# Scaled xi copied to PSUM by TensorE as the source of ScalarE's products, in a kernel of pairwise outer products with batch normalization

## The chip, the cores and the metric

The kernel runs on one core of a Trainium2 chip. Its metric is the device time of one execution in microseconds. The times below are of three executions and of one more under the hardware profiler. "ACT" is ScalarE, "DVE" VectorE, "PE" TensorE, "POOL" GpSimd and "SP" SyncE, which issues all stores.

## The reference

There are two inputs xi and xj of 1024 x 39 x 16, a 16 x 16 weight W, and gamma and beta of 741 entries. For every pair of fields (row r, column c) with c < r, 741 pairs in all, and for every batch element, the outer product of xj's field r and xi's field c is formed, normalized by mean and variance over the batch and over its 256 entries, scaled and shifted, and multiplied by W element by element. The output is 1024 x 1 x 741 x 16 x 16 in fp32, 776.99 MB.

```python
cross = xj[:, rows, :, None] * xi[:, cols, None, :]
mean = jnp.mean(cross, axis=(0, 2, 3), keepdims=True)
var = jnp.mean(jnp.square(cross - mean), axis=(0, 2, 3), keepdims=True)
normed = (cross - mean) * jax.lax.rsqrt(var + BN_EPS)
normed = normed * gamma[None, :, None, None] + beta[None, :, None, None]
out = normed[:, :, None, :, :] * W[None, None, :, :, :]
```

## The kernel before

**Layout.** Batch element 8p + t lies on partition p, so there are eight values of t on each of 128 partitions. A *tile* is one row r (or two short rows) for two values of t: 2r pairs of 256 entries on each partition. `y_sb` holds 152 pairs and is reused in turn: a tile's products can only be written where earlier stores have landed. The tuple of a tile in `FIRST` and `LAPS` (L19 to L32) is: the rows; how many of the 16 values of i POOL multiplies instead of ACT; how many pairs ("share") POOL finishes instead of DVE; whether ACT adds the shift for that share (1) or POOL (0); and how many pairs DVE finishes ahead for the first t alone. The 120 tiles are numbered in the order of the code: 0 to 3 are row 19, 4 to 11 rows 20 and 18 in turn, 12 to 15 row 38, and from 16 on longer rows come with short ones.

**Statistics.** Sixteen loads of 312 KB, one of them in two parts, bring in xi and xj; sums and squares on DVE, ACT, POOL and PE (L376 to L411) give two small matrices, from which scale and shift of all pairs follow (L476 to L489). PE spreads them over the partitions by matmuls (`spread`, L496, into PSUM), and `apply` (L512, three DVE operations a group) multiplies in gamma and adds beta, group of rows by group of rows (`ROW_GROUPS`, L46). A group is applied four tiles (group 2: three) before its first use (L537 to L540).

**The steps of a tile n.** `scale_xi` (L186, POOL, L193) multiplies xi by the scale into `xs`, of which there are two buffers. `products` (L201) forms xs times xj[i] for each of 16 values of i and each t: ACT does i below `split` (L170), POOL the others (L172); rows up to 5 go to POOL at once (L228), rows up to 4 to DVE (L209, L219). `finish` (L282) adds the shift and multiplies by W: POOL for its share (shift at L298 by ACT or L300 by POOL, weight at L303), DVE for all other pairs in one operation each (L319). `store` (L241) then sends the tile, or one t of it, to the output from SP (L246). Tile 1 (`RAW`) has a share of its own, `POOL_PAIRS_RAW` (L38), and the first three tiles a number of i of their own, `POOL_I_FIRST`.

**The order** is written out by hand (`manual_schedule`): for n = 1, 2, ... it is scale_xi(n + 2), finish(n), the groups that are due, products(n + 1). Each engine runs its instructions in that order.

**PSUM.** One bank holds W for DVE (`w_dve`), seven are `banks`; the first serve the statistics and, from tile 12 on, xj of the short rows (`xj_short`, ScalarE's copy at L551); the others hold the spread groups.

Of the kernel before, what the change touches and what calls it, by code (L numbers as in the profile page):

```python
# [7 lines left out]
F32 = mybir.dt.float32  # L8
# [6 lines left out]
T = 2  # L15
# [2 lines left out]

FIRST = ((19,), 5, 3, 0, 0)  # L19
LAPS = (  # L20
# [14 lines left out]
)  # L35


POOL_I_FIRST, POOL_PAIRS_RAW = (6, 6, 5), 2  # L38

SHORT, OWN = 4, 1  # L40


OUTER = 5
# [4 lines left out]
    (5, 10, 2), (25, 29, 3), (10, 14, 3), (21, 25, 4), (14, 18, 4),  # L48
)
SHORT_GROUP = 5  # L50


@with_exitstack
def tile_pair_outer_batchnorm(
# [15 lines left out]
    nc = tc.nc  # L70
    P = nc.NUM_PARTITIONS
    NB, F, E = xi.shape
    NT = NB // P
    EE = E * E
    NP = F * (F - 1) // 2
    first = [r * (r - 1) // 2 for r in range(F)]

# [4 lines left out]
    tiles = [(FIRST, t0, t0 // T * half // 2) for t0 in range(0, NT, T)]  # L82
    for lap in LAPS:
        size = T * sum(sum(member[0]) for member in lap)
# [12 lines left out]
    cpool = ctx.enter_context(tc.tile_pool(name="cpool", bufs=1))  # L97
    scaled_short = ctx.enter_context(tc.tile_pool(name="scaled_short", bufs=1))
    scaled = ctx.enter_context(tc.tile_pool(name="scaled", bufs=2))
    psp = ctx.enter_context(tc.tile_pool(name="ps", bufs=1, space=bass.MemoryType.PSUM))  # L100
    xi_sb = cpool.tile([P, NT, F, E], F32, name="xi_sb")
    xj_sb = cpool.tile([P, NT, F, E], F32, name="xj_sb")
    w_sb = cpool.tile([P, 1, EE], F32, name="w_sb")
    st_sb = cpool.tile([P, 2, NP], F32, name="st_sb")
    s_sb = st_sb[:, 0:1].unsqueeze(3)
    t_sb = st_sb[:, 1]
    y_sb = cpool.tile([P, 2 * half, EE], F32, name="y_sb")
    w_dve = psp.tile([P, 1, EE], F32, name="w_dve")

    xi_v = xi.rearrange("(p t) f e -> p t f e", t=NT)  # L110
    xj_v = xj.rearrange("(p t) f e -> p t f e", t=NT)
    out_v = out.rearrange("(p t) o n i j -> p t (o n i j)", t=NT)


# [1 line left out]
    flat = y_sb.rearrange("p n e -> p (n e)")  # L116
    place = {"mid": half // 2 * EE, "dev": half * EE, "rest": (half + half // 2) * EE}
    stop = {"mid": half * EE, "dev": (half + half // 2) * EE, "rest": 2 * half * EE}

    def scratch(part, parts, *shape):  # L120
        size = 1
        for n in shape:
            size *= n
        at = place[part]
        place[part] = at + size
        assert place[part] <= stop[part]
        ap = flat[0:parts, at : at + size]
        if len(shape) == 2:
            ap = ap.rearrange("p (a b) -> p a b", b=shape[1])
        elif len(shape) == 3:  # L130
            ap = ap.rearrange("p (a b c) -> p a b c", b=shape[1], c=shape[2])
        return ap

    G = F - 1
    H = E // 2
    squares = [scratch("dev", P, NT, G, E) for _ in range(2)]
    halves = [[scratch("mid", P, NT, G, H) for _ in range(2)] for _ in range(2)]
    ones = scratch("rest", P, P)  # L140
    unit = scratch("rest", P, P)
    pick = scratch("rest", G, G, P)
    moments = [scratch("rest", P, NT, 2 * G) for _ in range(2)]
    squared, low, rstd, inv = (scratch("rest", G, G) for _ in range(4))
    stq = scratch("rest", G, 2, G)
    banks = [psp.tile([P, 512], F32, name=f"ps{n}") for n in range(7)]
    ps_s, ps_c, ps_g = banks[0], banks[1], banks[2:5]

    xj_short = ps_c.rearrange("p (t r i) -> p t r i", t=NT, i=E)

    ps_st = banks[5:7] + ps_g
    stt = nc.vector.scalar_tensor_tensor
# [1 line left out]
    def view(n):  # L154
        (rows, *_), _, u = tiles[n]
        return y_sb[:, u : u + T * sum(rows), :].rearrange("p (t n) e -> p t n e", t=T)

    def parts(n):
        at = 0
        for r in tiles[n][0][0]:  # L160
            yield r, at, at + r
            at += r

    def product(n, r, at, engine, t, i, src):

        t0 = tiles[n][1]
        y = view(n)[:, t, at : at + r].rearrange("p n (i j) -> p n i j", j=E)[:, :, i, :]
        scale = xj_sb[:, t0 + t, r, i : i + 1]
        if engine is nc.scalar:
            nc.scalar.activation(y, src, AF.Copy, scale=scale)  # L170
        else:
            engine.tensor_scalar(y, src, scale, 1.0, ALU.mult, ALU.mult)  # L172
# [13 lines left out]
    def scale_xi(n):  # L186
# [11 lines left out]
            )  # L198
        xs_of[n] = xs

    def products(n):  # L201

        t0 = tiles[n][1]
        xs = xs_of.pop(n, None)
        for r, c0, c1 in parts(n):
            outer = view(n)[:, :, c0:c1].rearrange("p t n (i j) -> p t n i j", j=E)
            if r <= SHORT:
                xs_r = scaled_short.tile([P, T, r, E], F32, tag="xs_short", name=f"xs_{r}_{t0}")
                nc.vector.tensor_tensor(  # L209
                    xs_r,  # L210
                    xi_sb[:, t0 : t0 + T, 0:r, :],
                    s_short[:, first[r] : first[r] + r]
                    .unsqueeze(1)
                    .unsqueeze(3)
                    .to_broadcast([P, T, r, E]),
                    ALU.mult,
                )
                for t in range(T):
                    nc.vector.tensor_tensor(  # L219
                        outer[:, t],  # L220
                        xs_r[:, t].unsqueeze(2).to_broadcast([P, r, E, E]),
                        xj_short[:, t0 + t, r - 1 : r, :].unsqueeze(3).to_broadcast([P, r, E, E]),
                        ALU.mult,
                    )
                continue
            if r <= OUTER:
                for t in range(T):
                    nc.gpsimd.tensor_tensor(  # L228
                        outer[:, t],
                        xs[:, t, c0:c1].unsqueeze(2).to_broadcast([P, r, E, E]),  # L230
                        xj_sb[:, t0 + t, r : r + 1, :].unsqueeze(3).to_broadcast([P, r, E, E]),
                        ALU.mult,
                    )
                continue
            split = E - (POOL_I_FIRST[n] if n < len(POOL_I_FIRST) else tiles[n][0][1])
            for t in range(T):
                for i in range(E):
                    engine = nc.scalar if i < split else nc.gpsimd
                    product(n, r, c0, engine, t, i, xs[:, t, c0:c1])

    def store(n, c0, c1, t_from=0, t_to=T):  # L241
        (rows, *_), t0, _ = tiles[n]
# [2 lines left out]
        for t in range(t_from, t_to, step):  # L245
            nc.sync.dma_start(  # L246
                out_v[:, t0 + t : t0 + t + step, (n0 + c0) * EE : (n0 + c1) * EE],
                view(n)[:, t : t + step, c0:c1, :].rearrange("p t n e -> p t (n e)"),
# [85 lines left out]
    with tc.manual_schedule():  # L334
        nc.gpsimd.memset(ones, 1.0)  # L335

        def load(engine, to, source, t):
            engine.dma_start(to[:, t], source[:, t])

        nc.sync.dma_start(xi_sb[:, 0, 0 : F // 2], xi_v[:, 0, 0 : F // 2])  # L340
        nc.scalar.dma_start(xi_sb[:, 0, F // 2 : F], xi_v[:, 0, F // 2 : F])
        load(nc.sync, xj_sb, xj_v, 0)
        load(nc.scalar, xi_sb, xi_v, 1)
        load(nc.sync, xj_sb, xj_v, 1)
# [19 lines left out]

        sources = (xj_sb[:, :, 1:F], xi_sb[:, :, 0:G])
        scales = (0.25, 0.25 / NB**0.5)

        def field(x, k):  # L370
# [103 lines left out]
        scale = 1.0 / (NB * EE)  # L474
# [18 lines left out]
        spread_of = []  # L493
# [18 lines left out]
        def apply(group):  # L512
            ps, n0, n1 = spread_of[group]
            nc.vector.tensor_mul(ps[:, 1], ps[:, 1], st_sb[:, 0, n0:n1])
            if group == SHORT_GROUP:

                nc.vector.tensor_mul(ps[:, 0], ps[:, 0], st_sb[:, 0, n0:n1])
                nc.vector.tensor_copy(st_sb[:, 0, n0:n1], ps[:, 0])
            else:
                nc.vector.tensor_mul(st_sb[:, 0, n0:n1], ps[:, 0], st_sb[:, 0, n0:n1])  # L520
            nc.vector.tensor_add(st_sb[:, 1, n0:n1], ps[:, 1], st_sb[:, 1, n0:n1])

        spread(0)
        apply(0)

        affine(0, range(OWN, 12))
# [2 lines left out]
        weigh(0)  # L529
        for group in range(1, len(ROW_GROUPS)):  # L530
            spread(group)
        s_short = spread_of[SHORT_GROUP][0][:, 0]
        apply(1)
        products(1)
        scale_xi(2)

        due = {}  # L537
        for group, (r0, r1, _) in enumerate(ROW_GROUPS[2:], 2):
            use = min(n for n, tile in enumerate(tiles) if any(r0 <= r < r1 for r in tile[0][0]))
            due.setdefault(use - 3 if group == 2 else use - 4, []).append(group)  # L540

        for n in range(1, len(tiles)):
            if n + 2 < len(tiles):
                scale_xi(n + 2)
            finish(n)
            for group in due.get(n, ()):
                apply(group)
            if n + 1 < len(tiles):
                products(n + 1)
            if n == 12:  # L550
                nc.scalar.copy(xj_short, xj_sb[:, :, 1 : SHORT + 1, :])  # L551


# [26 lines left out]
```

## Time and profile before

| | us |
|---|---|
| median of 3 runs | 1863.21 |
| lowest and highest | 1863.09, 1863.3 |
| the profiled execution, its own time | 1863.2 |
| its span in the profile | 1861.1 |

| engine | busy us | share of the span |
|---|---|---|
| DVE | 1764.1 | 95% |
| POOL | 1593.2 | 86% |
| ACT | 1581.5 | 85% |
| PE | 33.1 | 2% |
| DMA queue of SP (16 DMA engines) | | 98.6% |

The mean rate of the DMA is 421 GB/s over the span: 6.00 MB are read and 776.99 MB written. The costliest groups are DVE's finish at L319 (3014 operations, 1703.0 us), ACT's products at L170 (3000, 1453.8 us) and POOL's products at L172 (1192, 635.9 us) and weights at L303 (131, 531.4 us).

A group's line gives the busy time, the mean of one operation in ns, and the idle time of its engine just before such operations with what ended it. A line of the waits gives who waited for whom: us in total, how often, the longest. A line of the operations in order of time gives start, length, engine, line, operation, how many are merged, and in brackets the idle time before. A line of a table by stretches gives, after the stretch, each engine's busy time with the number of operations (PE, PE's weight loads, DVE, ACT, POOL), PE's granted clock, the DMA's share and GB/s.

### The profile page before, as it was taken

The page shows a single profiled execution, that of the slowest core. Times are in us where ns is not written, and L with a number is a line of the kernel's source. Part 1 is how long each engine was busy: PE and PEld are TensorE (multiplying, and loading weights), DVE is VectorE, ACT ScalarE, POOL GpSimd, SP SyncE. Part 2 cuts the span into 40 slices and gives each one's busy share as a digit, 9 for nine tenths or more (in the row PEclk, how much of TensorE's full clock was granted, in tenths as well). Part 3 has the DMA queues.
Part 4 walks back from the last instruction along what each step waited for, and adds up shares of the span by engine and source line. Part 5 has one row for each costly group of instructions (what it writes and reads, how often), then busy time and mean ns, then how long its engine had stood idle before and what let it go on. Part 6 is the DMA issues. An engine that isn't in the chain of part 4 may idle for free. (4 is left out here: it accounts for less than half of the span.)

```text
span 1861.1 us, 10096 instructions
## 1 busy us (share of the span) xinstructions
PE 33.1 (2%) x212; PEld 32.3 (2%) x212; DVE 1764.1 (95%) x3141; ACT 1581.5 (85%) x3208; POOL 1593.2 (86%) x1810
## 2 busy tenths in 40 slices
PE   7000000000000000000000000000000000000000
PEld 6000000000000000000000000000000000000000
DVE  8999999998999999999999999899999999999894
ACT  8999888888888777779888888888888888888991
POOL 9989878888888799989888888999988888888791
PEclk7555555555555555555555555555555555555555
DMA  7999999999999999999999999999999999999998
GB/s 290 393 422 418 440 427 429 430 436 413 429 436 430 423 427 429 428 431 427 428 429 429 428 433 431 429 406 429 427 423 427 424 425 428 414 424 425 427 427 369
DMA packets 41356, 783.64 MB, mean 421 GB/s; under 512 B 4288, under 2 KB 4928, under 8 KB 11712
## 3 DMA queue, kind: packets, MB, share of 16 engines
q1 hardware_dynamic: 40992, 782.53, 98.6%
q14 instruction: 75, 0.61, 0.1%
q10 hardware_dynamic: 288, 0.48, 0.1%
q8 instruction: 1, 0.02, 0.0%
HBM read 6.00 MB, written 776.99 MB: 421 GB/s over the span
## 5 line engine op out<-in xcount | busy, mean ns | idle before, releaser
L319 DVE SCALAR_TENSOR_TENSOR y_sb<-y_sb,st_sb,w_dve 128x512 f32<-128x512 f32 (+1 forms) x3014 | 1703.0, 647 | 61.7 <-POOL y_sb L172 48.1
L170 ACT ACTIVATE y_sb<-xs,xj_sb 128x576 f32<-128x576 f32 (+23 forms) x3000 | 1453.8, 576 | 227.6 <-DMA out_dram<-y_sb 198.3
L172 POOL TENSOR_SCALAR y_sb<-xs,xj_sb 128x112 f32<-128x112 f32 (+27 forms) x1192 | 635.9, 557 | 6.2 <-DMA out_dram<-y_sb 4.9
L303 POOL TENSOR_TENSOR y_sb<-y_sb,w_sb 128x2048 f32<-128x2048 f32 (+4 forms) x131 | 531.4, 4063 | 71.3 <-ACT y_sb L298 63.7
L193 POOL TENSOR_TENSOR xs<-xi_sb,st_sb 128x640 f32<-128x640 f32 (+33 forms) x135 | 182.9, 1362 | 148.2 <-ACT y_sb L170 130.9
L300 POOL TENSOR_SCALAR y_sb<-y_sb,st_sb 128x512 f32<-128x512 f32 x300 | 202.2, 691 | 2.0 <-ACT y_sb L170 2.0
L298 ACT ACTIVATE y_sb<-y_sb,st_sb 128x512 f32<-128x512 f32 x168 | 105.1, 708 | 4.6 <-POOL y_sb L172 3.1
L219 DVE TENSOR_TENSOR y_sb<-xs,ps 128x256 f32<-128x256 f32 (+3 forms) x32 | 24.8, 817 | 0.5
L228 POOL TENSOR_TENSOR y_sb<-xs,xj_sb 128x1280 f32<-128x1280 f32 x8 | 18.7, 2364 | 0.0
L503 PE MATMUL ps<-y_sb 38*128 38x38 f32 (+37 forms) x76 | 15.3, 379 | 2.4 <-DVE y_sb L489 2.4
L503 PEld LDWEIGHTS ps<-y_sb 38*128 38x128 f32 x76 | 15.2, 310 | 2.5 <-POOL y_sb L172 2.5
L172 POOL TENSOR_SCALAR y_sb<-xi_sb,xj_sb 128x304 f32<-128x304 f32 x24 | 11.9, 515 | 0.0
L269 DVE TENSOR_TENSOR y_sb<-y_sb,w_dve 128x2048 f32<-128x2048 f32 (+4 forms) x6 | 10.8, 1840 | 0.5 <-POOL y_sb L262 0.5
L380 DVE TENSOR_REDUCE y_sb<-y_sb 128x38 f32<-128x608 f32 x14 | 10.4, 780 | 0.0
L262 POOL TENSOR_SCALAR y_sb<-y_sb,st_sb 128x512 f32<-128x512 f32 x9 | 7.0, 791 | 1.5 <-ACT y_sb L170 1.5
L377 ACT ACTIVATE y_sb<-xj_sb 128x608 f32<-128x608 f32 x8 | 5.7, 709 | 1.2 <-DMA xj_sb<-in_r_xj_dram 0.6
L377 ACT ACTIVATE y_sb<-xi_sb 128x608 f32<-128x608 f32 x8 | 5.7, 709 | 1.1 <-DMA xi_sb<-in_r_xi_dram 0.7
L260 ACT ACTIVATE y_sb<-y_sb,st_sb 128x512 f32<-128x512 f32 x9 | 6.5, 800 | 0.1
L395 PE MATMUL ps<-xi_sb,y_sb 128*128 128x152 f32 x40 | 5.8, 293 | 0.3 <-DMA xi_sb<-in_r_xi_dram 0.3
L417 PE MATMUL ps<-y_sb 128*128 128x128 f32 x24 | 5.4, 426 | 1.0 <-POOL y_sb L335 1.0
L395 PEld LDWEIGHTS ps<-xi_sb,y_sb 128*128 128x128 f32 x40 | 5.4, 190 | 0.5 <-issue 0.5
L380 DVE TENSOR_REDUCE y_sb<-xi_sb 128x38 f32<-128x608 f32 x2 | 1.6, 785 | 3.9 <-DMA xi_sb<-in_r_xi_dram 3.9
(43 smaller groups left out, 54.1 us busy)
## 6 DMA issues: line engine op xcount, KB each, us to landing
out_dram<-y_sb SPq DMA_DIRECT2D x16, 3968.0 KB, 19.5
out_dram<-y_sb SPq DMA_DIRECT2D x16, 3456.0 KB, 20.9
out_dram<-y_sb SPq DMA_DIRECT2D x16, 2944.0 KB, 20.3
out_dram<-y_sb SPq DMA_DIRECT2D x8, 4864.0 KB, 16.8
out_dram<-y_sb SPq DMA_DIRECT2D x8, 4736.0 KB, 18.4
out_dram<-y_sb SPq DMA_DIRECT2D x8, 4608.0 KB, 20.2
out_dram<-y_sb SPq DMA_DIRECT2D x8, 4480.0 KB, 17.0
out_dram<-y_sb SPq DMA_DIRECT2D x8, 4352.0 KB, 17.7
```

The source lines that it names most:

```text
L170: nc.scalar.activation(y, src, AF.Copy, scale=scale)
L172: engine.tensor_scalar(y, src, scale, 1.0, ALU.mult, ALU.mult)
L193: nc.gpsimd.tensor_tensor(xs[:, :, c0:c1, :], xi_sb[:, t0 : t0 + T, 0:r, :], s_sb[:, :, n0 : n0 + r, :].to_broadcast([P, T, r, E]), ALU.mult,)
L219: nc.vector.tensor_tensor(outer[:, t], xs_r[:, t].unsqueeze(2).to_broadcast([P, r, E, E]), xj_short[:, t0 + t, r - 1 : r, :].unsqueeze(3). ...
L228: nc.gpsimd.tensor_tensor(outer[:, t], xs[:, t, c0:c1].unsqueeze(2).to_broadcast([P, r, E, E]), xj_sb[:, t0 + t, r : r + 1, :].unsqueeze(3 ...
L298: nc.scalar.activation(y[:, :, c, :], y[:, :, c, :], AF.Identity, bias=t_c)
L300: nc.gpsimd.tensor_scalar(y[:, :, c, :], y[:, :, c, :], t_c, 1.0, ALU.add, ALU.mult)
L303: nc.gpsimd.tensor_tensor(y[:, :, c0:c1, :], y[:, :, c0:c1, :], w_sb.unsqueeze(1).to_broadcast([P, T, c1 - c0, EE]), ALU.mult,)
L319: stt(y[:, t0:t1, c, :], y[:, t0:t1, c, :], t_sb[:, n0 + c : n0 + c + 1], w_dve.to_broadcast([P, t1 - t0, EE]), ALU.add, ALU.mult,)
L377: nc.scalar.activation(squares[x][:, t], sources[x][:, t], AF.Square, scale=scales[x])
L380: nc.vector.tensor_reduce(moment(x, k, t, t + 1), field(x, k)[:, t : t + 1], AX.X, ALU.add)
L503: nc.tensor.matmul(ps[:, :, first[r] - n0 : first[r] - n0 + r], pick[:, r - 1, :], stq[:, :, 0:r], start=True, stop=True,)
```

## The change

The source of ACT's products moves from SBUF to PSUM for tiles 2 and on with rows over 5. A new function `near` multiplies the identity matrix `unit` with `xs[:, t]` on PE, in pieces of at most 512 columns, into a PSUM area of that t (`wide[t]`), and ACT reads it there; POOL goes on reading `xs` in SBUF. Up to tile 11 an area is one bank; at `WIDE` = 10 the four banks of the pool `psq` are given back, and two areas of two banks each take their place. Row groups 3 to 7 are applied earlier (`DUE`: at tiles 7, 7, 8, 11 and 12, as against 8, 12, 14, 36 and 38), the scale of the short rows moves into W's bank, and `xj_short` into another bank, copied at tile 14 instead of 12.

Shares: rows 20 and 18 give POOL one i less in the products and one pair more to finish (3, 3 to 2, 4 and 4, 2 to 3, 3); tile 1 gives POOL one pair instead of two. Of xi the fields 0 to 37 and of xj the fields 1 to 38 are loaded, 38 of each instead of 39; the identity gets a place of its own.

```diff
-    (((20,), 3, 3, 0, 0), ((18,), 4, 2, 0, 0),),
+    (((20,), 2, 4, 0, 0), ((18,), 3, 3, 0, 0),),
...
-POOL_I_FIRST, POOL_PAIRS_RAW = (6, 6, 5), 2
+POOL_I_FIRST, POOL_PAIRS_RAW = (6, 6, 5), 1
...
+NEAR, WIDE = 2, 10
...
+DUE = {2: 2, 3: 7, 4: 7, 5: 8, 6: 11, 7: 12}
...
-    w_dve = psp.tile([P, 1, EE], F32, name="w_dve")
-    xi_v = xi.rearrange("(p t) f e -> p t f e", t=NT)
-    xj_v = xj.rearrange("(p t) f e -> p t f e", t=NT)
+    w_bank = psp.tile([P, 512], F32, name="w_bank")
+    w_dve = w_bank[:, 0:EE].unsqueeze(1)
+    s_short = w_bank[:, EE : EE + SHORT * (SHORT + 1) // 2]
+    unit = cpool.tile([P, P], F32, name="unit")
+    xi_v = xi[:, 0:G].rearrange("(p t) f e -> p t f e", t=NT)
+    xj_v = xj[:, 1:F].rearrange("(p t) f e -> p t f e", t=NT)
...
-    banks = [psp.tile([P, 512], F32, name=f"ps{n}") for n in range(7)]
+    lasting = [psp.tile([P, 512], F32, name=f"ps{n}") for n in range(3)]
+    early = ExitStack()
+    psq = early.enter_context(tc.tile_pool(name="psq", bufs=1, space=bass.MemoryType.PSUM))
+    passing = [psq.tile([P, 512], F32, name=f"psq{n}") for n in range(4)]
+    banks = passing[0:2] + lasting + passing[2:4]
+    wide = [b[:, :] for b in banks[0:2]]
...
+    def near(n, xs, t, c0, c1):
+        size = (c1 - c0) * E
+        bank = wide[t]
+        flat_xs = xs[:, t, c0:c1].rearrange("p n e -> p (n e)")
+        for a in range(0, size, 512):
+            b = min(a + 512, size)
+            nc.tensor.matmul(bank[:, a:b], unit, flat_xs[:, a:b], start=True, stop=True)
+        return bank[:, 0:size].rearrange("p (n e) -> p n e", e=E)
...
+        skip = sum(r for r in tiles[n][0][0] if r <= OUTER)
+        xs_act = {}
+        if n >= NEAR and tiles[n][0][0][-1] > OUTER:
+            for t in range(T):
+                xs_act[t] = near(n, xs, t, skip, sum(tiles[n][0][0]))
...
                 for i in range(E):
-                    engine = nc.scalar if i < split else nc.gpsimd
-                    product(n, r, c0, engine, t, i, xs[:, t, c0:c1])
+                    if i >= split:
+                        product(n, r, c0, nc.gpsimd, t, i, xs[:, t, c0:c1])
+                    elif t in xs_act:
+                        product(n, r, c0, nc.scalar, t, i, xs_act[t][:, c0 - skip : c1 - skip])
+                    else:
+                        product(n, r, c0, nc.scalar, t, i, xs[:, t, c0:c1])
...
-            due.setdefault(use - 3 if group == 2 else use - 4, []).append(group)
+            due.setdefault(DUE.get(group, use - 4), []).append(group)
...
-            if n == 12:
-                nc.scalar.copy(xj_short, xj_sb[:, :, 1 : SHORT + 1, :])
+            if n == WIDE:
+                early.close()
+                psw = ctx.enter_context(tc.tile_pool(name="psw", bufs=1, space=bass.MemoryType.PSUM))
+                wide[:] = [psw.tile([P, 1024], F32, name=f"wide{t}") for t in range(T)]
+            if n == 14:
+                nc.scalar.copy(xj_short, xj_sb[:, :, 0:SHORT, :])
```

More of the change, by code (lines that the diff above doesn't have):

```diff
@@ L74, in tile_pair_outer_batchnorm @@
     EE = E * E
+    G = F - 1
     NP = F * (F - 1) // 2
@@ L100, in tile_pair_outer_batchnorm @@
     psp = ctx.enter_context(tc.tile_pool(name="ps", bufs=1, space=bass.MemoryType.PSUM))
-    xi_sb = cpool.tile([P, NT, F, E], F32, name="xi_sb")
-    xj_sb = cpool.tile([P, NT, F, E], F32, name="xj_sb")
+    xi_sb = cpool.tile([P, NT, G, E], F32, name="xi_sb")
+    xj_sb = cpool.tile([P, NT, G, E], F32, name="xj_sb")
     w_sb = cpool.tile([P, 1, EE], F32, name="w_sb")
@@ L132, in scratch @@
         return ap
-    G = F - 1
     H = E // 2
@@ L140, in tile_pair_outer_batchnorm @@
     ones = scratch("rest", P, P)
-    unit = scratch("rest", P, P)
     pick = scratch("rest", G, G, P)
@@ L145, in tile_pair_outer_batchnorm @@
     stq = scratch("rest", G, 2, G)
-    banks = [psp.tile([P, 512], F32, name=f"ps{n}") for n in range(7)]
+    lasting = [psp.tile([P, 512], F32, name=f"ps{n}") for n in range(3)]
[4 more added lines that the diff above has]
+    wide = [b[:, :] for b in banks[0:2]]
     ps_s, ps_c, ps_g = banks[0], banks[1], banks[2:5]
-    xj_short = ps_c.rearrange("p (t r i) -> p t r i", t=NT, i=E)
+    xj_short = ps_g[0].rearrange("p (t r i) -> p t r i", t=NT, i=E)
     ps_st = banks[5:7] + ps_g
@@ L167, in product @@
         y = view(n)[:, t, at : at + r].rearrange("p n (i j) -> p n i j", j=E)[:, :, i, :]
-        scale = xj_sb[:, t0 + t, r, i : i + 1]
+        scale = xj_sb[:, t0 + t, r - 1, i : i + 1]
         if engine is nc.scalar:
@@ L230, in products @@
                         xs[:, t, c0:c1].unsqueeze(2).to_broadcast([P, r, E, E]),
-                        xj_sb[:, t0 + t, r : r + 1, :].unsqueeze(3).to_broadcast([P, r, E, E]),
+                        xj_sb[:, t0 + t, r - 1 : r, :].unsqueeze(3).to_broadcast([P, r, E, E]),
                         ALU.mult,
@@ L338, in load @@
             engine.dma_start(to[:, t], source[:, t])
-        nc.sync.dma_start(xi_sb[:, 0, 0 : F // 2], xi_v[:, 0, 0 : F // 2])
-        nc.scalar.dma_start(xi_sb[:, 0, F // 2 : F], xi_v[:, 0, F // 2 : F])
+        nc.sync.dma_start(xi_sb[:, 0, 0 : G // 2], xi_v[:, 0, 0 : G // 2])
+        nc.scalar.dma_start(xi_sb[:, 0, G // 2 : G], xi_v[:, 0, G // 2 : G])
         load(nc.sync, xj_sb, xj_v, 0)
@@ L361, in tile_pair_outer_batchnorm @@
         )
-        sources = (xj_sb[:, :, 1:F], xi_sb[:, :, 0:G])
+        sources = (xj_sb, xi_sb)
         scales = (0.25, 0.25 / NB**0.5)
@@ L515, in apply @@
             if group == SHORT_GROUP:
-                nc.vector.tensor_mul(ps[:, 0], ps[:, 0], st_sb[:, 0, n0:n1])
-                nc.vector.tensor_copy(st_sb[:, 0, n0:n1], ps[:, 0])
+                nc.vector.tensor_mul(s_short, ps[:, 0], st_sb[:, 0, n0:n1])
+                nc.vector.tensor_copy(st_sb[:, 0, n0:n1], s_short)
             else:
@@ L531, in tile_pair_outer_batchnorm @@
             spread(group)
-        s_short = spread_of[SHORT_GROUP][0][:, 0]
         apply(1)
```

## The prediction

> **What bounds the kernel now.** I read the page first (shares of the span, the slices, the DMA queues), then the waits, then the operations in order of time, and last the completions that the trace holds for every store.
>
> ```profile
> span 1861.1 us, 10096 instructions
> PE 33.1 (2%) x212; PEld 32.3 (2%) x212; DVE 1764.1 (95%) x3141; ACT 1581.5 (85%) x3208; POOL 1593.2 (86%) x1810
> ...
> DMA  7999999999999999999999999999999999999998
> ...
> q1 hardware_dynamic: 40992, 782.53, 98.6%
> q14 instruction: 75, 0.61, 0.1%
> ```
>
> The stores fill the DMA: 98.6% of sixteen engines' span, nine tenths or more in every slice but the first and last. DVE is 95% busy beside it, but nothing says that it ends later. The waits say who waits for whom:
>
> ```profile
> ACT y_sb L170 <- DMA out_dram<-y_sb: 198.3, 87, 5.2
> POOL xs L193 <- ACT y_sb L170: 130.9, 42, 6.5
> ```
>
> ScalarE idles 198.3 us in 87 waits for a store to free its part of y_sb, so over most of the run ACT has time to spare. There is one stretch where it has none:
>
> ```profile
> 29.68 8.87 ACT L170 ACTIVATE y_sb<-xs,xj_sb 128x304 f32<-128x304 f32 x20
> 38.76 122.58 ACT L170 ACTIVATE y_sb<-xs,xj_sb 128x304 f32<-128x304 f32 x266 [0.21 <-POOL xs L193]
> 161.44 5.01 ACT L298 ACTIVATE y_sb<-y_sb,st_sb 128x512 f32<-128x512 f32 x8
> ```
>
> From 29.7 to 166.5 us ACT works without a break (tiles 1 to 12), the chain then passes to GpSimd:
>
> ```profile
> 164.07 9.03 POOL L303 TENSOR_TENSOR y_sb<-y_sb,w_sb 128x2048 f32<-128x2048 f32 x2 [0.32 <-ACT y_sb L298]
> ```
>
> That ends at 173.10, and the first store of tile 12 (row 38, store number 32 counted from 0) is issued at 173.73. Its packets start at 174.9. I call this store the gate. After the gate the DMA alone sets the pace, and more exactly one DMA engine does. Each store has sixteen completions in the trace, one per DMA engine. At the store issued at 1194.1 fifteen are within 3.15 us of the median (1204.68) and the last is 7.40 behind; at the final store the median is 1855.05 and the last 1860.06. Wherever the late engine's packets can be told from the others' by their size (some 55 stretches after 920 us) each begins 3 to 13 ns before the one ahead of it ends: it never idles. The others do:
>
> ```profile
> 240.00:260.00 20.00, 0.00 (x0) 0.00 (x0) 18.21 (x39) 16.37 (x26) 12.62 (x12) 0.50 1.01 434
> ...
> 440.00:460.00 20.00, 0.00 (x0) 0.00 (x0) 14.32 (x29) 18.82 (x31) 18.51 (x13) 0.50 0.93 395
> 1200.00:1220.00 20.00, 0.00 (x0) 0.00 (x0) 20.00 (x32) 18.47 (x49) 18.39 (x30) 0.50 0.90 386
> 1600.00:1620.00 20.00, 0.00 (x0) 0.00 (x0) 18.00 (x32) 19.12 (x42) 19.75 (x26) 0.50 0.93 396
> ```
>
> The last two columns are DMA share and GB/s. At 1214 the other engines lose some 2 us, and just there the late one's lag falls from 7.4 to 5.2: they wait, it catches up, and the end stays where it was. Its own sum: first completion 27.08, all further packets at 38.1 ns per KB (19,456 B take 724 to 728 ns) 1806.2, excess 26.7, together 1860.0. Of the excess 7.0 is spent by 74 us (stores that come late, DVE-paced), 2.2 by 134, 17.5 later, about 1 us for each 92 us.
>
> **What the Trainium skill says.** "Perfetto Trace Analysis", Optimizing Scalar/DVE Operations: a ScalarE instruction pays about 93 ns for access to SBUF and about 51 to PSUM. The trace agrees as far as it goes: a 38x38 ACTIVATE from PSUM (L476) takes 197 ns, one of that shape from SBUF (L483) 235, so 38 less. "ScalarE: Activation LUTs", What ACT_TABLE_LOAD costs: 0.833 ns per element, about 93 ns for a pointer operand, and neighbours overlap by about 93. Agrees: 304 elements take 533 ns and start 438 apart. "PSUM — Partial Sum Buffer", PSUM bank collisions: two engines may not be in one bank at once, so TensorE may write a bank only when ACT has left it. In the changed program each such copy does wait for ACT.
>
> **The change part by part.** Against the profiled execution (span 1861.1, own time 1863.2, so 2.1 around it; median of the runs 1863.21).
>
> (a) *38 fields.* A load shrinks from 2496 to 2432 B a partition, 0.13 MB in all, 0.3 us at 404 GB/s. DVE is 4.92 and 5.00 busy of 5 us while they land, so the statistics do not end sooner: 0 to -0.3, I take -0.05.
>
> (b) *ACT's source is PSUM, tiles 2 on.* ACT's path to the gate now: tiles 2 and 3 44 products at 438 ns, tiles 4 to 11 26 at 451 and 24 at 425 in turn, tile 12 22 at 691; 19.3+87.7+15.3 = 122.3 (seen: 122.58). The new shares give ACT 28 and 26: 94.7 instead of 87.7. Each of the 282 products saves d. Two hops to TensorE lie open. Tile 2 can't be copied before its xs is done (38.73): by L417 (12 products of 128 columns, each two records, in 5.44 us, 3.5 ns a column) 304 columns take 1.1 us; with weights and signal I take 1.65. At tile 12 the two-bank tiles lie on the four banks that tile 11 used, so the copy begins when ACT has finished: 608 columns, 2.15, with the rest 2.6. Later hops hide: one t's bank is filled while ACT is at the other t (7 us). New end: 38.76+1.65+19.3+94.7+2.6+15.3 = 172.3 less 282 d. With d = 37 ns 161.9, with 42 160.5; now 161.34. Bounds: d = 0 gives 172.3 (+11), d = 42 -0.9. I take d = 37: gate +0.5.
>
> (c) *Shares.* DVE has one pair less in each of tiles 4 to 11 (658 ns, 5.3 us together), one more in tile 1. Pool: tile 1 loses one L300 (0.69) and half of a 2.35 L303, so it no longer makes DVE wait at 48.66; ACT's hop does (tile 2's products end at about 49.3 instead of 48.5), and tile 3 starts at about 60.5 as now. A 20-row tile costs Pool 2.1+2.8+4.5+1.3 = 10.7, an 18-row one 9.5, both under ACT's 11.6 and 10.1. DVE reaches tile 12 some 3 us sooner and then waits for ACT and Pool: 0 at the gate.
>
> (d) *Row groups earlier.* Three small DVE operations each (0.93 us for 142 columns); three groups more before the gate, 2.4 us, paid from (c). 0. If that cover were gone the gate would move by them.
>
> (e) *xs freed by TensorE.* L193's 130.9 us of waiting goes; Pool starts shares up to 6.5 us sooner, which fills holes such as the one at 1214. Worth nothing while the late DMA engine sets the end.
>
> (f) *Fetches.* 268 more matmuls are 1072 more records on TensorE (106 are 212 and 212 now), with their waits some 1240 instructions. 10096 instructions go with 75 fetches, so 9 or 10 more, 309 ns each on one DMA engine. Of seven that fall into the stretches where the late engine is alone, one lengthened its packet (1244 for 954). If TensorE's share its engine: +2.9; if not: 0. I take +0.2.
>
> Sum: the late engine is free at 174.63 and the gate's packets start at 174.9, so the gate decides already now; a later one costs in full, an earlier one gives 0.26 at most. +0.5 from ACT, -0.05 from the loads, +0.2 from (f), and -0.2 for a late store at 126 us that the quicker DVE brings forward: **+0.4, 1863.6 us**.
>
> **The rivals.** *The holes count* (1855): if all sixteen engines bound together, the holes after 120 us (packets in flight fewer than sixteen, summed in the trace: 10 us) would be worth having, and (e) with faster ACT would give back about 8. For: three windows at 0.90 to 0.93. Against: the late engine has no gap. *ACT gets no relief* (1874): d is near 0, because the fixed part overlaps with the neighbour anyhow. Then ACT ends tile 12 at 172.3; the gate opens 12.4 us after that (161.34 to 173.73 now), 11 us later, and nothing behind it makes that good, since the DMA is full from there. For: the measured 38 ns are of single instructions, none back to back. Against: the fixed 185 ns between starts (438 less 253 for the elements) hold an access that PSUM shortens. Each ns of d is 0.28 us: the gate is later than now from d under 39 on, by over 0.2% from d under 25 on. *TensorE's fetches fall on the late engine* (1866.3): the sum of (f), spread over the run. *The change does not do what it says*, copies in the open at every tile: 110 tiles at over 1 us would exceed any slack, but the order of the program lets them run a tile ahead; part of the second rival.
>
> **How the numbers follow.** Forecast 0.66 (its own range 1862.3 to 1864.8), fetches on the late engine 0.16, no relief for ACT 0.09, holes 0.09. The range takes in the first two with d from 34 to 42: 1861.8 to 1867.0. About 0.2% (3.7 us) is what can be told from no change: faster 0.09, same 0.80, slower 0.11.
>
> **What would show it.** ACT's product of 304 elements near 495 ns, starts 401 apart; first PSUM product near 40.4; tile 12's products ended near 162; store 32 issued near 174.2; L193's waits gone; holes at 450 and 1214 smaller, while the last engine still ends each store 5 to 8 us late and the end stays. Wrong if the last engine's excess after 134 us falls under 16, or the gate moves by over 2 us.

## The result, and the profile after

The changed kernel takes 1866.55 us (median of 19 runs, 1866.30 to 1867.31), against 1863.30 (19 runs, 1863.06 to 1864.02) in the same session. The ratio is 1.0018, 95% interval 1.0011 to 1.0025: 3.25 us slower. The forecast was 1863.6, the range 1861.8 to 1867.0. The profiled execution has an own time of 1866.55 and a span of 1864.5, where before had 1863.2 and 1861.1.

The page after, the lines that answer to those shown of before (q14 and q8 carry the fetches of instructions; q8 had 1 packet of 16,384 B before):

```profile
span 1864.5 us, 11299 instructions
PE 417.9 (22%) x748; PEld 173.1 (9%) x748; DVE 1760.3 (94%) x3134; ACT 1486.8 (80%) x3224; POOL 1598.3 (86%) x1801
...
DMA  7999999999999999999999999999999999999998
...
q1 hardware_dynamic: 40992, 782.42, 98.4%
q14 instruction: 75, 0.61, 0.1%
...
q8 instruction: 6, 0.10, 0.0%
```

ScalarE is 94.7 us less busy and TensorE 384.8 us more; the DMA is as full as it was, for 3.4 us longer. There are 1203 more instructions. The waits (us in total, times, longest):

```profile
ACT y_sb L181 <- DMA out_dram<-y_sb: 270.7, 103, 5.5
...
POOL xs L204 <- DVE st_sb L550: 0.6, 1, 0.6
```

GpSimd's 130.9 us of waiting for ScalarE (L193 before, L204 now) are gone, and ScalarE waits 72.4 us longer for stores: most of what it saved after the gate became waiting. Up to the gate, ScalarE's and GpSimd's operations in order of time:

```profile
29.57 8.88 ACT L181 ACTIVATE y_sb<-xs,xj_sb 128x304 f32<-128x304 f32 x20
40.10 105.36 ACT L181 ACTIVATE y_sb<-psq,xj_sb 128x304 f32<-128x304 f32 x260 [1.65 <-PE psq L218]
148.14 14.58 ACT L181 ACTIVATE y_sb<-wide,xj_sb 128x608 f32<-128x608 f32 x22 [2.68 <-POOL xs L204]
162.81 5.01 ACT L327 ACTIVATE y_sb<-y_sb,st_sb 128x512 f32<-128x512 f32 x8
```

```profile
165.45 9.01 POOL L332 TENSOR_TENSOR y_sb<-y_sb,w_sb 128x2048 f32<-128x2048 f32 x2 [2.19 <-ACT y_sb L327]
```

The two waits for TensorE in the open are there, 1.65 and 2.68 us. (The second line names GpSimd, whose operation ended at 147.92; TensorE's copy for this tile, begun at 145.56 when ScalarE had left the banks, ended at 147.97.) Tile 12's products end at 162.72 (161.34 before), GpSimd at 174.46 (173.10), and store 32 is issued at 174.48 (173.73). So GpSimd's chain came 1.36 us later and the store 0.75. The rest had been hidden: before, it was VectorE that held this store last. It worked there without a break,

```profile
126.11 50.30 DVE L319 SCALAR_TENSOR_TENSOR y_sb<-y_sb,st_sb,w_dve 128x512 f32<-128x512 f32 x86
```

and its last operation for the store ended at 173.67, 0.57 after GpSimd; after, VectorE is done at 172.52 and GpSimd is the last. The windows:

```profile
240.00:260.00 20.00, 4.76 (x8) 2.35 (x8) 16.11 (x36) 16.38 (x26) 13.39 (x12) 0.50 1.01 436
440.00:460.00 20.00, 0.88 (x3) 0.33 (x1) 14.51 (x28) 17.84 (x30) 18.10 (x13) 0.50 0.99 421
1200.00:1220.00 20.00, 5.17 (x6) 1.51 (x6) 19.24 (x30) 17.66 (x54) 19.12 (x30) 0.50 0.83 355
1600.00:1620.00 20.00, 6.66 (x8) 1.57 (x7) 20.00 (x35) 16.25 (x37) 19.75 (x26) 0.50 0.80 343
```

The hole near 450 shrank (DMA share 0.99, was 0.93), those at 1200 and 1600 grew (0.83 and 0.80, were 0.90 and 0.93). Still each packet of the late DMA engine begins 3 to 13 ns before the one ahead of it ends. Its sum from the completions, "excess" being what exceeds 38.1 ns per KB, and "instructions" those that ended in the stretch:

| part of the late engine's time, us | before | after | difference |
|---|---|---|---|
| first completion | 27.08 | 26.98 | -0.10 |
| excess, stores 1 to 31 | 9.62 | 9.23 | -0.39 |
| excess, store 32 (the gate) | 0.00 | 1.23 | +1.23 |
| excess, stores 33 to 96 | 3.28 | 4.27 | +0.99 |
| excess, stores 97 to 247 | 13.83 | 15.50 | +1.67 |
| last completion | 1860.06 | 1863.45 | +3.39 |
| instructions, stores 33 to 96 | 2387 | 2771 | +384 |
| instructions, stores 97 to 247 | 6184 | 6845 | +661 |

The gate accounts for +0.74 (first three rows). The other 2.66 us come evenly: from store 97 on the end of each dozen stores is some 0.14 us later than the dozen before would make it. The number of 8192-byte fetches in that part is 48 in both; of the new ones of 16,384 bytes three lie there, in stores 106, 155 and 218, whose excess is within 0.03 us of what it was before.

### The profile page after: what moved, and what is told of

Read it like the earlier page. It is cut to its first block, busy times and chain, and to the rows that moved or that the text cites. A ratio compares the mean times of both kernels' runs of the same rounds, so it can differ in the third digit from the quotient of the medians.

```text
span 1864.5 us, 11299 instructions
## 1 busy us (share of the span) xinstructions
PE 417.9 (22%) x748; PEld 173.1 (9%) x748; DVE 1760.3 (94%) x3134; ACT 1486.8 (80%) x3224; POOL 1598.3 (86%) x1801
## 4 chain that ended last, share of the span: by engine, by line
DMA 51%; ACT 27%; DVE 14%; POOL 2%; issue 1%; PE 0%; ACTq 0%; SPq 0%; DVEq 0%; POOLq 0%
DMA out_dram<-y_sb 51%; ACT y_sb L181 26%; DVE y_sb L348 14%; ACT y_sb L327 1%; POOL y_sb L183 1%; POOL y_sb L332 1%; POOL y_sb L329 0%; POOL xs L204 0%; PE wide L218 0%; ACTq L181 0%; SPq L275 0%; DVEq L607 0%; ACTq L607 0%; DVEq L348 0%; DVE xs L234 0%
## 5 line engine op out<-in xcount | busy, mean ns | idle before, releaser
L348 DVE SCALAR_TENSOR_TENSOR y_sb<-y_sb,st_sb,w_bank 128x512 f32<-128x512 f32 (+1 forms) x3007 | 1698.9, 648 | 68.1 <-issue 33.9
L181 ACT ACTIVATE y_sb<-wide,xj_sb 128x496 f32<-128x496 f32 (+26 forms) x2736 | 1244.9, 680 | 321.3 <-DMA out_dram<-y_sb 270.7
L183 POOL TENSOR_SCALAR y_sb<-xs,xj_sb 128x576 f32<-128x576 f32 (+25 forms) x1176 | 628.7, 559 | 43.3 <-DMA out_dram<-y_sb 29.4
L218 PE MATMUL wide<-xs,unit 128*128 128x512 f32 (+13 forms) x496 | 357.8, 846 | 1318.2 <-ACT y_sb L181 1053.9
L332 POOL TENSOR_TENSOR y_sb<-y_sb,w_sb 128x2048 f32<-128x2048 f32 (+5 forms) x131 | 538.4, 4117 | 79.3 <-ACT y_sb L327 71.7
L218 PEld LDWEIGHTS wide<-xs,unit 128*128 128x128 f32 x496 | 130.6, 314 | 1545.5 <-ACT y_sb L181 545.9
L204 POOL TENSOR_TENSOR xs<-xi_sb,st_sb 128x640 f32<-128x640 f32 (+33 forms) x135 | 182.9, 1363 | 8.2 <-DVE st_sb L550 0.6
L181 ACT ACTIVATE y_sb<-psq,xj_sb 128x320 f32<-128x320 f32 (+2 forms) x260 | 105.4, 1579 | 1.6 <-PE psq L218 1.6
L218 PE MATMUL psq<-xs,unit 128*128 128x320 f32 (+2 forms) x40 | 27.0, 783 | 72.1 <-ACT y_sb L181 71.0
L532 PE MATMUL ps<-y_sb 38*128 38x58 f32 (+25 forms) x52 | 11.3, 399 | 0.0
L298 DVE TENSOR_TENSOR y_sb<-y_sb,w_bank 128x2048 f32<-128x2048 f32 (+4 forms) x6 | 10.8, 1840 | 0.5 <-POOL y_sb L291 0.5
```

The lines of the kernel that those rows point to most:

```text
L204: nc.gpsimd.tensor_tensor(xs[:, :, c0:c1, :], xi_sb[:, t0 : t0 + T, 0:r, :], s_sb[:, :, n0 : n0 + r, :].to_broadcast([P, T, r, E]), ALU.mult,)
L218: nc.tensor.matmul(bank[:, a:b], unit, flat_xs[:, a:b], start=True, stop=True)
L298: nc.vector.tensor_tensor(y[:, :, c0:c1, :], y[:, :, c0:c1, :], w_dve.unsqueeze(1).to_broadcast([P, T, c1 - c0, EE]), ALU.mult,)
L332: nc.gpsimd.tensor_tensor(y[:, :, c0:c1, :], y[:, :, c0:c1, :], w_sb.unsqueeze(1).to_broadcast([P, T, c1 - c0, EE]), ALU.mult,)
L348: stt(y[:, t0:t1, c, :], y[:, t0:t1, c, :], t_sb[:, n0 + c : n0 + c + 1], w_dve.to_broadcast([P, t1 - t0, EE]), ALU.add, ALU.mult,)
L532: nc.tensor.matmul(ps[:, :, first[r] - n0 : first[r] - n0 + r], pick[:, r - 1, :], stq[:, :, 0:r], start=True, stop=True,)
```

## The experiments

All ran beside runs of the kernel before (medians 1863.37 to 1863.38). *Theory I* is that each instruction, on whatever engine, takes a few ns of the late DMA engine; its rivals are that the copies' data cost the time (*D*), and that the gate and the times at which buffers come free do (*G*).

**Copies that nobody reads**, against the changed kernel:

```diff
-    (((20,), 2, 4, 0, 0), ((18,), 3, 3, 0, 0),),
+    (((20,), 3, 3, 0, 0), ((18,), 4, 2, 0, 0),),
-POOL_I_FIRST, POOL_PAIRS_RAW = (6, 6, 5), 1
+POOL_I_FIRST, POOL_PAIRS_RAW = (6, 6, 5), 2
-                        product(n, r, c0, nc.scalar, t, i, xs_act[t][:, c0 - skip : c1 - skip])
+                        product(n, r, c0, nc.scalar, t, i, xs[:, t, c0:c1])
```

> The changed kernel, with ScalarE reading its products' source from SBUF again and with the old shares of rows 19, 20 and 18; TensorE still makes every copy, and nobody reads them. Theory I (every instruction, on whatever engine, takes some 2.25 ns of one DMA engine, the late one: the traces of before and after give 13.83 us for 6184 instructions and 15.50 for 6845 from store 97 on): about 1000 more instructions after the gate, so +2.3 us, 1865.6, with the late engine's excess from store 97 on at about 15.5 us, and the gate where it was (store 32 issued near 173.7). Theory D (the copies' data cost, TensorE's reads of SBUF beside the DMA's): the same here, 1865.6. Theory G (the change costs by what ScalarE and GpSimd do, that is by the gate and the times at which buffers come free): 1863.3, excess 13.8.

Measured: 1867.63 us, ratio 1.0023 (1.0014 to 1.0031). Excess from store 97 on 15.29. After the gate the expected 2.3 us came (2.35 at the last store); but the gate, expected unmoved, was 1.96 late at store 32's completion. GpSimd's chain to it ended on time, at 172.81, so VectorE was the late one: the changed dates of the row groups are in this kernel too, and the old shares leave VectorE no slack for them.

**The same copies, 16 columns wide**, against the one above:

```diff
-            nc.tensor.matmul(bank[:, a:b], unit, flat_xs[:, a:b], start=True, stop=True)
+            nc.tensor.matmul(bank[:, a : a + 16], unit, flat_xs[:, a : a + 16], start=True, stop=True)
```

> As copies_unused, but each copy only 16 columns wide instead of up to 512: the number of instructions stays, the data falls to about a twentieth. Theory I: 1865.6 and an excess of about 15.5 us from store 97 on, as for copies_unused. Theory D: 1863.4 and 13.9. Theory G: 1863.3 and 13.8.

Measured: 1867.59 us, ratio 1.0022 (1.0013 to 1.0030). Excess 15.26. The groups of the wide kernel, then of the narrow one:

```profile
L218 PE MATMUL wide<-xs,unit 128*128 128x512 f32 (+13 forms) x496 | 327.8, 823 | 1351.7 <-POOL xs L204 1351.7
```

```profile
L218 PE MATMUL wide<-xs,unit 128*128 128x16 f32 x496 | 124.0, 379 | 1555.5 <-POOL xs L204 1555.5
```

The matmuls are less than half as long and copy a small part of the data, and the time is the same within 0.04 us. D falls for the copied columns. The identity is still loaded as weights for each matmul; that this isn't needed for the effect is seen in the run with GpSimd's small operations below.

**Copies for tiles 2 to 12 only**, against the changed kernel:

```diff
-        if n >= NEAR and tiles[n][0][0][-1] > OUTER:
+        if NEAR <= n < 13 and tiles[n][0][0][-1] > OUTER:
```

> The changed kernel with copies for tiles 2 to 12 alone; from tile 13 on ScalarE reads SBUF as before the change. Theory I: the gate stays as late as in the changed kernel (store 32 issued near 174.5, +0.75 us), while the late engine's excess from store 97 on falls back to 13.8 us: 1864.1. Theory D: the same. Theory G: the gate's part stays and the rest depends on when buffers come free: between 1864 and 1866.5 with no reason for the excess to fall back.

Measured: 1863.84 us, ratio 1.0002 (0.9994 to 1.0010). Excess 13.82: with 6183 instructions in place of 6845 the whole rise of the late part is gone, and the gate's part stays (store 32 issued at 174.73, its completion 0.98 later than before). G falls for all but the gate.

**Small operations on GpSimd**, against the kernel before:

```diff
+    spare = cpool.tile([P, 1], F32, name="spare")
...
             finish(n)
+            for _ in range(8 if n >= 13 else 0):
+                nc.gpsimd.memset(spare, 0.0)
```

> The kernel before, with eight one-element memsets on GpSimd ahead of each tile's due groups from tile 13 on: 856 more instructions, no more data, nothing on TensorE. Theory I: +856 x 2.25 ns = +1.9 us, 1865.2, with an excess of 13.8 + 1.2 to 1.4 = about 15.1 us from store 97 on. A variant of it in which only TensorE's instructions count: 1863.3 and 13.8. Theory D: 1863.3. If GpSimd's own delay (8 small operations a tile) shows, the holes of the other DMA engines grow, and the end moves only where a hole is longer than the late engine's lag.

Measured: 1867.09 us, ratio 1.0020 (1.0012 to 1.0028); expected was 1865.2. Excess from store 97 on 15.81, +1.98 for 603 more instructions, which is 3.3 ns each instead of 2.25. The rest, +2.1 before store 97, comes mostly at stores 65 to 89, where GpSimd's delay (84.3 us of memsets in all) made stores late while the late engine had little lag to hide it (0.1 to 1.3 us). From store 97 on the median engine falls another 3.6 us behind its times of before, through holes, and the end shows only the late engine's 1.98. TensorE is not needed for the effect.

**The row groups' dates alone**, against the kernel before:

```diff
+DUE = {2: 2, 3: 7, 4: 7, 5: 8, 6: 11, 7: 12}
-            due.setdefault(use - 3 if group == 2 else use - 4, []).append(group)
+            due.setdefault(DUE.get(group, use - 4), []).append(group)
```

> The kernel before with the changed dates of the row groups alone (groups 3 to 7 applied at tiles 7, 7, 8, 11 and 12). In the run with unused copies and old shares the gate came 1.99 us late, with GpSimd's chain to it on time (172.79) and VectorE's late. Theory V (VectorE has no slack before the gate under the old shares, so the three groups that now lie before it, 2.57 us in that trace, cost nearly all): gate +1.5 to +2.0, 1865.1 to 1865.4; no more instructions, so the late engine's excess from store 97 on stays at 13.8. Theory P (TensorE's copies themselves delayed that gate): gate 173.7, 1863.4.

Measured: 1865.22 us, ratio 1.0010 (1.0002 to 1.0018). VectorE's last operations ahead of the gate, then SyncE's issue of store 32:

```profile
159.94 0.31 DVE L515 TENSOR_TENSOR ps<-ps,st_sb 128x155 f32<-128x155 f32 x1
160.28 0.32 DVE L521 TENSOR_TENSOR st_sb<-ps,st_sb 128x155 f32<-128x155 f32 x1
160.52 0.31 DVE L522 TENSOR_TENSOR st_sb<-ps,st_sb 128x155 f32<-128x155 f32 x1
160.74 15.69 DVE L320 SCALAR_TENSOR_TENSOR y_sb<-y_sb,st_sb,w_dve 128x256 f32<-128x256 f32 x31
```

```profile
176.10 0.33 SPq L247 DMA_DIRECT2D out_dram<-y_sb  x1
```

GpSimd is done at 173.16, as before; VectorE works without a break until the store is issued, 2.37 us later than before. The last completion is 2.32 later (1.84 by the medians of the time). The excess from store 97 on is 13.83, unmoved. Theory V holds, though the gate moved by more than the 1.5 to 2.0 us that it gave.

**The new shares alone**, against the kernel before: the two share lines of the change.

```diff
-    (((20,), 3, 3, 0, 0), ((18,), 4, 2, 0, 0),),
+    (((20,), 2, 4, 0, 0), ((18,), 3, 3, 0, 0),),
-POOL_I_FIRST, POOL_PAIRS_RAW = (6, 6, 5), 2
+POOL_I_FIRST, POOL_PAIRS_RAW = (6, 6, 5), 1
```

> The kernel before with the new shares of rows 19, 20 and 18 alone: ScalarE has 16 more products before the gate, 8 at 451 and 8 at 425 ns, 7.0 us, and no copies relieve it. If ScalarE's path sets the gate, the gate comes 7.0 us late (store 32 issued near 180.7), and all of it stays to the end: 1870.3. Then the copies are worth about 6 us at the gate in the changed kernel. If the late DMA engine's queue covers part of it (it is free at 175.1), 0.9 less at most; if GpSimd or VectorE set the gate, 1863.4 to 1866.

Measured: 1870.86 us, ratio 1.0040 (1.0027 to 1.0052). ScalarE's products of tile 12 end at 168.29 (+6.95), store 32 is issued at 181.65 (+7.92), the last completion is 8.02 later. A late gate does stay to the end in full, and in the changed kernel, which has the new dates as well, the copies are worth about 7.2 us at the gate (181.65 less 174.48).

**Copies for tiles 3 to 11 only**, against the changed kernel:

```diff
-NEAR, WIDE = 2, 10
+NEAR, WIDE = 3, 10
-        if n >= NEAR and tiles[n][0][0][-1] > OUTER:
+        if NEAR <= n < 12 and tiles[n][0][0][-1] > OUTER:
```

> The changed kernel with copies for tiles 3 to 11 alone: neither of the two waits for TensorE in the open (1.65 us at tile 2, 2.68 at tile 12) is left, and there are no copies after the gate. ScalarE's products of tile 12 should end near 160 (with 34 ns saved on each product of tiles 3 to 11), GpSimd's chain near 172.5, store 32 be issued near 173.0, that is before the late engine is free (174.6): the gate is covered. Theory I: excess from store 97 on 13.8, end 0.4 to 0.5 us earlier than before: 1862.9, faster than both kernels. If the holes or buffers of later tiles matter instead: 1863.4 or more.

Measured: 1862.59 us (13 runs, 1862.30 to 1863.11; before 25 runs, 1863.13 to 1863.93), ratio 0.9996 (0.9987 to 1.0004). ScalarE in order of time, then GpSimd:

```profile
38.91 9.77 ACT L181 ACTIVATE y_sb<-xs,xj_sb 128x304 f32<-128x304 f32 x22 [0.22 <-POOL xs L204]
48.58 96.56 ACT L181 ACTIVATE y_sb<-psq,xj_sb 128x304 f32<-128x304 f32 x238
143.12 17.18 ACT L181 ACTIVATE y_sb<-xs,xj_sb 128x608 f32<-128x608 f32 x22
```

```profile
163.26 9.02 POOL L332 TENSOR_TENSOR y_sb<-y_sb,w_sb 128x2048 f32<-128x2048 f32 x2 [0.32 <-ACT y_sb L327]
```

No wait in the open is left, tile 12 ends at 160.30, store 32 is issued at 172.31, and the late engine goes from store 31 (175.04) to 32 without a gap: the gate is covered. This is the fastest version of the study that forms the whole output: 3.96 us under the changed kernel, and 0.79 under before by the medians and without overlap of the runs, though the interval of the ratio reaches past 1. In the profiled executions the last completion is only 0.15 earlier (1859.91). Another 0.33 lies outside the profiled span (own time less span 1.72, before 2.05), and the two executions lie 0.12 above and 0.18 below their medians; why the time outside the span is shorter stays open. A faster kernel than before is therefore likely, not shown.

**The same with more for GpSimd in tiles 2 and 3**, against that kernel:

```diff
-FIRST = ((19,), 5, 3, 0, 0)
+FIRST = ((19,), 4, 4, 0, 0)
-POOL_I_FIRST, POOL_PAIRS_RAW = (6, 6, 5), 1
+POOL_I_FIRST, POOL_PAIRS_RAW = (6, 6, 4), 1
```

> The kernel with copies for tiles 3 to 11, and in tiles 2 and 3 one pair more finished by GpSimd and one value of i more multiplied by ScalarE. In the trace of the former the DMA is empty before the stores number 12 and 14 (56.1 and 66.7), which VectorE issues late, 1.85 and 1.9 us of the late engine's excess. VectorE loses one operation of 0.65 us in each of tiles 2 and 3: if it alone sets those stores, they come 0.65 and 1.3 us earlier and the end comes about 1 us earlier, 1861.5; GpSimd gains 1.8 us and loses 1.0 in each tile, and if it is the later one there, nothing is gained or some 0.5 us is lost: 1862.6 to 1863.1.

Measured: 1864.15 us, ratio 1.0004 (0.9996 to 1.0013), 1.56 over the former, more than either case expected. VectorE then waits 0.96 us for ScalarE ahead of tile 3 (not at all in the former) and 2.21 for GpSimd ahead of tile 4 (0.80); store 14 is issued at 68.20 instead of 66.75. VectorE alone did not set those stores.

**Half of ScalarE's products left out**, against the kernel before:

```diff
+                    if n >= 13 and i < split and i % 2 == 1:
+                        continue
```

> The kernel before, with every second of ScalarE's products (odd i) left out from tile 13 on, so that those parts of the output are not formed; all stores, and all work on VectorE, GpSimd and TensorE, stay. About 1270 instructions fewer after the gate, some 980 of them from store 97 on. Theory I: the late engine's excess from store 97 on falls from 13.8 to about 11.6 us, and the end by about 2.5 to 2.9 us, to 1860.5 to 1860.9. Theory that the late engine is slow by itself, with the same excess for each byte: 13.8, 1863.4. Theory that waiting for ScalarE (holes) matters: faster too, but with the excess from store 97 on unchanged.

Measured: 1858.66 us, ratio 0.9976 (0.9966 to 0.9985). Excess from store 97 on 10.16 for 5150 instructions: -3.67 for 1034 fewer, 3.55 ns each, more than expected. An engine that is slow by itself, by the same amount for each byte, is ruled out. Though ScalarE is far from any limit here (52% busy), the late engine alone still sets the end, 6.49 us behind the median.

**The last stores cut by partitions**, against the kernel before:

```diff
-            nc.sync.dma_start(
-                out_v[:, t0 + t : t0 + t + step, (n0 + c0) * EE : (n0 + c1) * EE],
-                view(n)[:, t : t + step, c0:c1, :].rearrange("p t n e -> p t (n e)"),
-            )
+            cuts = (0, P)
+            if n == len(tiles) - 1:
+                cuts = (0, 64, P) if t == 0 else (0, 120, P)
+            for a, b in zip(cuts, cuts[1:]):
+                nc.sync.dma_start(
+                    out_v[a:b, t0 + t : t0 + t + step, (n0 + c0) * EE : (n0 + c1) * EE],
+                    view(n)[a:b, t : t + step, c0:c1, :].rearrange("p t n e -> p t (n e)"),
+                )
```

> The kernel before with the last tile's two stores cut by partitions: the first into 64 and 64, the last into 120 and 8. A look at which partitions the late engine serves. If it serves the last 8 of 128 rows and the cut of 120 leaves it out, the last store's end falls by up to 4 us, to 1859.5; if the cut spreads the rows evenly or the late engine serves others, the end stays within 0.5 us of 1863.4.

Measured: 1871.92 us, ratio 1.0046 (1.0033 to 1.0060), 8.5 us slower, outside both cases. The last four stores end at 1856.14, 1863.42, 1868.58 and 1865.52. Between 1844 and 1855 us a packet of 17,408 bytes of these pieces takes 1.36 us in the median, where those of the uncut stores take 0.65. Why, and which rows the late engine serves, stays open; how to take load off it is therefore open too.

Theory I, all runs together. Stores 97 to 247 carry the same bytes in each kernel:

| kernels | instructions | late engine's excess, us |
|---|---|---|
| half of ScalarE's products left out | 5150 | 10.16 |
| before, and five others without copies there or memsets | 6182 to 6184 | 13.80 to 13.83 |
| unused copies, wide and narrow | 6761 | 15.29, 15.26 |
| memsets on GpSimd | 6787 | 15.81 |
| after | 6845 | 15.50 |

Fetches can't make these differences except in two runs: those of 8192 bytes are 48 in that part in every run but the one with half of the products left out (40) and the one with the memsets (53), and there a share of theirs is not excluded. Nor does the whole excess go with instructions. Each run holds lumps of about 0.6 us at the same three places, stores 138 to 139, 190 to 191 and 239 to 240 (in nine of eleven runs a fetch is seen beside the second). They are the same in all runs; the rest comes to some 2.0 ns an instruction, and to 1.5 in the first run of the table.

The packets show the same more closely. In eleven of these traces 2248 packets of the late engine after the gate can be told from the others' by their size and have no fetch beside them. Each is compared with the shortest of its size, by the number of instructions that ended while it ran, on any engine (97 packets with more than seven are left out of the table):

| instructions ended within the packet | packets | mean lengthening, ns |
|---|---|---|
| 0 | 94 | 0.2 |
| 1 | 114 | 4.7 |
| 2 | 207 | 5.8 |
| 3 | 389 | 9.2 |
| 4 | 633 | 10.7 |
| 5 | 397 | 12.7 |
| 6 | 196 | 16.6 |
| 7 | 121 | 17.0 |

A fit by engine gives 2.5 +- 0.2 ns for one of ScalarE, 2.7 +- 0.2 VectorE, 1.7 +- 0.2 GpSimd, 1.5 +- 0.3 SyncE and 2.3 +- 0.2 TensorE (standard errors). Theory I is what the runs and the packets show. What the engine carries for the instructions is not shown. Every execution here was recorded, so whether it is the instructions or the recording of them can't be told apart by these runs.

## Why the prediction was right and where it failed

The time fell into the range, and the sign of the forecast's small rise was right, but most of it came by a mechanism to which it gave 0.2 of its 0.4 us. The change measured +3.25, outside the forecast's own range (1862.3 to 1864.8); the wider range held it because it took in the rival *TensorE's fetches fall on the late engine* (1866.3, chance 0.16). That rival had the right engine and the wrong carrier; that 9 or 10 fetches of 309 ns come near to what some 1000 instructions cost is luck.

- *What bounds the kernel* held in every run but the one with the last stores cut: the gate, and after it one DMA engine. A gate 7.92 us late cost 8.02 at the end; 3.6 us of further holes on the other engines, in the run with memsets, cost nothing beside the late engine's excess.
- *(a) Loads*, -0.05: the first completion came 0.10 earlier, but it varies by as much between kernels that don't touch the loads (1.07 later in one run). Not decided.
- *(b) ScalarE from PSUM*, gate +0.5: the two hops were right (1.65 forecast and seen; 2.6 against 2.68), d was not. With 37 ns tile 12 would have ended at 161.9, it ended at 162.72; (172.3 - 162.72) / 282 gives 34 ns. The Trainium skill ("Perfetto Trace Analysis", Optimizing Scalar/DVE Operations) has 93 against 51, that is 42; the single 38x38 operation showed 38; back to back it is 34, and that measurement is what the sum needs. Of the 1.38 us only 0.75 reached the gate, because VectorE had held it last before, 0.57 after GpSimd; the forecast moved the gate with ScalarE and left out that VectorE was the last. That +0.5 came near to +0.75 is two errors in opposite directions. The rival *ACT gets no relief* is refuted by the run with the new shares alone.
- *(c) and (d)*, 0 at the gate, with 2.4 to pay if the cover were gone: so it is. Alone the dates cost 2.32 us at the last completion, and in the changed kernel the new shares' eight pairs cover them: VectorE is done 1.94 us before GpSimd there.
- *(e)*: the 130.9 us went and bought nothing, as said. That the hole at 1214 would shrink was wrong: the other engines lost 3.3 us there, against 2.0 before. ScalarE now waits 2.3 us for a store there (0.2 before); that this is the cause wasn't tried. The end doesn't show it. The late engine's lag fell there from 7.5 to 5.0 us before (the prediction read 7.4 and 5.2) and from 9.7 to 5.6 after.
- *(f) Fetches*, +0.2, is the step that failed. It measured +2.66. I counted 9 or 10 fetches of 309 ns and asked whether such a lump falls on the late engine; in the profile of before one of seven did, and I took most of the cost away. The extra instructions brought no more 8192-byte fetches at all, but five of 16,384 bytes (q8), and the cost came evenly, about 2.5 ns for each added instruction: 1.67 us for 661 and 0.99 for 384. In the trace of before this was in view as "excess 17.5 after 134 us, about 1 us for each 92 us". I took it for a property of the engine and didn't ask what it goes with. 13.83 us over 6184 instructions would have given 2.24 ns each, and the 1045 more from store 33 on 2.3 us, within 0.4 of what came.
- *The falsifiers*: the gate moved by 0.75 (limit 2), and the excess after 134 us didn't fall under 16 but rose from 17.5 to 21.4. I had set no limit above.

Put together with the measured terms: 1863.2 + 0.74 (gate and loads) + 2.66 (instructions) = 1866.6, where the profiled execution took 1866.55.

## What to carry to other kernels

Where one DMA engine ends each transfer later than the rest and never idles, its excess is part of the kernel's time: divide it by the number of instructions in the same stretch, and charge a change for the instructions it adds on any engine, busy or not. All times here are of recorded executions, and whether unrecorded ones pay this is open. A relief for an engine is worth having only in the stretch where that engine sets the pace: here the copies paid up to the gate and cost 2.7 us behind it, and copies for tiles 3 to 11 alone made a kernel 3.96 us faster than the changed one. An edit that is free in company should be priced alone as well: the row groups' dates cost 2.3 us without the shares that came with them.

## What the runs showed of the hardware

The starts that the profile records for ScalarE's products with a PSUM source run ahead of the work:

```profile
L181 ACT ACTIVATE y_sb<-psq,xj_sb 128x320 f32<-128x320 f32 (+2 forms) x260 | 105.4, 1579 | 1.6 <-PE psq L218 1.6
```

The 260 take 105.4 us in all, 405 ns each, but the mean length is given as 1579 ns: the recorded starts are 43 ns closer than those from SBUF, the ends 34 ns, and the difference adds up from product to product. For the saving, the ends are to be read. The per-instruction cost was not quite uniform by whole runs either: 2.5 ns for TensorE's copies, 3.3 for GpSimd's memsets, 3.55 for ScalarE's products; what makes the difference stays open. In the last two the number of fetches differs from the kernel before as well.
